# Another tile ring for the weights' transfers, and a later split, in a four-layer cross-attention kernel

## The chip, the cores and the metric

The kernel runs on one NeuronCore of one Trainium2 chip. The metric is the device time of one execution in microseconds (us), shown as a median of several runs. Work is spread over TensorE (PE; its weight loads are PEld), VectorE (DVE), ScalarE (ACT), GpSimd (POOL) and SyncE (SP), which here issues all transfers. Each engine works through its own list of instructions strictly in order; semaphores hold an instruction back until what it needs is there.

## The reference

Four transformer layers in a row work on `x` (32 batches of 112 rows, 256 wide, float32), and on a context `ctx` (32 x 375 x 256). Cut to what matters:

```python
def L0(x, kv):              # grouped attention, 16 heads of 64, 4 for keys and values
    return x + attend(rms(x) @ wq.T, rms(kv) @ wk.T, rms(kv) @ wv.T) @ wo.T
def L1(x, context):         # heads of 16, everything quantised to 8 bits
    x = attn_q(ln(x), ln(x)) + x
    x = attn_q(ln(x), context) + x
    a, g = split(ln(x) @ ff_w1 + ff_b1)
    return a * gelu(g) @ ff_w2 + ff_b2 + x
def L2(q, k, v):            # 16 heads of 64
    q1 = q + attend(ln(q) @ Wq, k @ Wk, v @ Wv) @ Wproj.T + bproj
    return q1 + relu(ln(q1) @ W1.T + b1) @ W2.T + b2
def L3(x_e, x):             # heads of 16, the first attention causal
    x = x + mha(ln(x), ln(x), causal=True) @ m_proj_w + m_proj_b
    x = x + mha(ln(x), x_e, causal=False) @ c_proj_w + c_proj_b
    return x + relu(ln(x) @ f_w1 + f_b1) @ f_w2 + f_b2
y = L3(ctx, L2(L1(L0(x, ctx), ctx), ctx, ctx))
```

## The kernel before

**Sweeps and slots.** Nine sweeps go over all 32 batches: `l0x`; `l1s`, `l1x`, `l1f`; `l2x`, `l2f`; `l3s`, `l3x`, `l3f` (s is self-attention, x cross-attention, f a feed-forward). `order` lays them out in pairs that overlap (l0x with l1s, l1x with l1f, l2x alone, l2f with l3s, l3x with l3f) as one list of 1672 slots. A slot is a small piece of a sweep: two heads of one batch in l0x, four heads in l3s, one eighth of the inner width for two batches in a feed-forward. `run` goes through the slots by their number k. At each it emits the slot's matrix products and, by `LAGS`, later stages of earlier slots; `fill` places projections, norms and loads ahead of their due slot.

**Two orders.** What `run` emits is a priority, not yet the order. When the program is built, a scheduler replays it against its own estimate of how long everything takes, and lets an instruction go early if its inputs and its tile are free and its engine has nothing more urgent. The result is a fixed list for each engine. `tc.issue_after(ins)` keeps what is traced inside it behind `ins` in the list of the engine that runs `ins`, and concerns no other engine.

**Tiles.** SBUF tiles come from rings, one for each tag, with the number of places given by `BUFS`: `xh` has 4, `s1` has 9, `k3` has 11, `w` (split weights) has 8. A tile of a ring has to wait until an older tile of it is given up. `xh` serves the norms: squares (L443), the normalised rows (L219, L475) and the scaled, transposed rows (L213, L215). `s1` serves the feed-forwards' inner sums `uu` (l1f, l2f, l3f), the quantised probabilities and their transposes in l1s, and the v tiles of l1s and l3s (two for each batch of l3s; L1018 clears them).

**Weights.** Matrix products are done as three passes on a high and a low part, so every weight has to be split. `wtile` (L302 on) cuts a weight into chunks of 128 x 256 float32, 128 KB each. For a chunk, `load` (L318) brings it into a raw tile: of `k3` for the first three weights of layer 0, of `xh` for all others. `cut` writes the high part into the `w` tile (`copy`, L202 on ACT, L204 on DVE or L206 on POOL, chosen by the `SHARE` tables) and the low part by a subtraction (L233, on DVE or POOL); for l3s's and l3x's query weights a scaling (L323) goes first. `run` loads one chunk for each slot (`load_w`) as soon as its `w` tile is free, and splits it (`cut_w`) at the next slot, just before the next load:

```python
                cut_w()
                for z in self.sweeps:
                    if wq[z]:
                        if not wq[z][0][0] or free_w > 0:
                            load_w(z)
                        break
```

By that rule layer 0's, l1s's and the first of l1x's weights are loaded in slots 0 to 31, l2f's 16 chunks in slots 767 to 776 and 1021 to 1028, l3s's and l3x's in 1029 to 1044, and l3f's 16 chunks in slots 1265 to 1280, where l2f ends, l3s runs until 1302 and l3x begins.

**Small loads.** `vec` and `scalar` queue the loads of bias and scale vectors in `self.early`; `vectors(2)` issues two of them for each of the slots 8 to 33, behind the last transfer of queries (`lastq`, L715). `self.then` holds four functions that need them: two of `deltas` (L1366 to L1368: reciprocals and products of quantisation steps, for l1s and l1x) and two scalings of query biases (L1389, for l3s and l3x). All four are emitted at slot 34. `load_biases`, at slot 40, writes a tile of zeros to memory, loads the eight output biases into one `xh` tile (L281), splits it (L282) and combines both parts into `biases`, which later products add with one more pass (L291).

Of the kernel before, what the change touches and what calls it, by code (L numbers as in the profile page):

```python
# [8 lines left out]
F32 = mybir.dt.float32  # L9
F32R = mybir.dt.float32r  # L10
# [11 lines left out]
D = 256  # L22
# [39 lines left out]
class Kern:  # L62
# [5 lines left out]
        l0x=[0, 1, 3, 4, 7],  # L68
        l1s=[0, 1, 3, 4, 5],
# [3 lines left out]
        l2f=[0, 0, 0, 0, 0],  # L73
        l3s=[0, 0, 1, 2, 2],
        l3x=[0, 1, 3, 4, 4],
        l3f=[0, 4, 1, 4, 3],
# [46 lines left out]
    def __init__(self, ctx, tc, A, out, B, sweeps):  # L123
        self.tc, self.nc, self.A, self.out, self.B = tc, tc.nc, A, out, B
        self.sweeps = sweeps
        self.uid = 0
        self.cp = ctx.enter_context(tc.tile_pool(name="cp", bufs=1))
        self.wp = ctx.enter_context(tc.tile_pool(name="wp", bufs=1))
        self.sp = ctx.enter_context(tc.tile_pool(name="sp", bufs=1))
        self.pp = ctx.enter_context(tc.tile_pool(name="pp", bufs=1, space=PSUM))  # L130
        self.dp = ctx.enter_context(tc.tile_pool(name="dp", bufs=1, space=DRAM))
        nc = self.nc
        self.turns, self.cur, self.wait = {}, None, None

        self.early, self.then, self.lastq = [], [], None

        self.dqs = {}
        c = lambda name, shape, dt: self.cp.tile(shape, dt, name=name, tag=name)
        self.ident = c("ident", [128, 128], F32)
        make_identity(nc, self.ident)  # L140
        self.identb = c("identb", [128, 128], BF16)
        make_identity(nc, self.identb)
        self.nhalf = c("nhalf", [128, 4], F32)
        nc.gpsimd.memset(self.nhalf, -0.5)
        self.magic = c("magic", [128, 1], F32)
        nc.gpsimd.memset(self.magic, MAGIC)
        self.evod = c("evod", [128, 2], F32)
        nc.gpsimd.memset(self.evod, 0.0)
        for e in range(2):
            nc.vector.tensor_reduce(  # L150
                self.evod[:, e : e + 1], self.ident.rearrange("p (a b d) -> p a b d", b=2, d=16)[:, :, e, :], AX.XY, ALU.add
            )

        self.biases = c("biases", [128, D], F32R)
        self.parity = c("parity", [128, 2], F32)
        self.pick = c("pick", [128, 8], F32R)
        pick = c("pick_", [128, 8], F32)
        nc.vector.tensor_reduce(pick, self.ident.rearrange("p (n b) -> p n b", b=2)[:, :8, :], AX.X, ALU.add)
        for e in range(2):
            nc.vector.tensor_reduce(self.parity[:, e : e + 1], self.ident.rearrange("p (n b) -> p n b", b=2)[:, :, e], AX.X, ALU.add)  # L160
        nc.vector.tensor_copy(self.pick, pick)

        own = c("own", [128, 8], F32)
        nc.vector.tensor_reduce(own, self.ident.rearrange("p (a d) -> p a d", d=16), AX.X, ALU.add)
        self.own = c("ownb", [128, 8], BF16)
        nc.vector.tensor_copy(self.own, own)
        self.mask = c("mask", [S, S], BF16)
        nc.gpsimd.memset(self.mask, 0.0)
        nc.gpsimd.affine_select(
            out=self.mask, in_=self.mask, pattern=[[-1, S]], base=0, channel_multiplier=1, compare_op=ALU.is_ge, fill=NEG  # L170
        )
# [98 lines left out]
    def load_biases(self):  # L270

        nc = self.nc
        self.zeros = self.dram([128, 8 * S], F32, "zeros", 1)
        z = self.t([128, 8 * S], F32, "h")
        nc.gpsimd.memset(z, 0.0)
        nc.sync.dma_start(self.zeros, z)
        raw, lo = self.t([128, D], F32, "xh"), self.t([128, D], F32, "xh")
        hi = self.t([128, D], F32R, "xh")
        nc.gpsimd.memset(raw, 0.0)
        for n, name in enumerate(self.BIAS.values()):  # L280
            nc.sync.dma_start(raw[2 * n : 2 * n + 2], self.A[name].partition_broadcast(2))  # L281
        self.split(raw, hi, lo)  # L282
        nc.vector.tensor_scalar(raw, hi.bitcast(F32), self.parity[:, 0:1], None, ALU.mult)
        nc.vector.scalar_tensor_tensor(self.biases, lo, self.parity[:, 1:2], raw, ALU.mult, ALU.add)
# [13 lines left out]

    FIRST = tuple("L0_xattn_" + n for n in ("wk", "wv", "wq"))


    def wtile(self, r, *parts):  # L302

        box = {}
        chunks = []
        o = 0
        for pi, (key, src, k0, kc, n0, n, *by) in enumerate(parts):
            by = by[0] if by else 1.0
            for q, m in [(q, m) for q in range(kc) for m in range(0, n, 256)]:

                def load(first=pi == 0 and q == 0 and m == 0, o=o, kc=kc, src=src, k=k0 + q, m=m, n0=n0, n=n):
                    if first:
                        self.uid += 1
                        box["w"] = self.wp.tile([128, 2048], F32R, tag="w", name=f"w_{self.uid}", bufs=self.BUFS["w"])
                    v = box["w"][:, o : o + kc * n * 2].rearrange("p (k h n) -> p k h n", k=kc, h=2)
                    a = self.A[src].rearrange("(k p) n -> p k n", p=128)
                    raw = self.t([128, 256], F32, "k3" if src in self.FIRST else "xh")
                    self.lastw = self.nc.sync.dma_start(raw, a[:, k, n0 + m : n0 + m + 256])  # L318
                    return v, raw

                def cut(v, raw, q=q, m=m, src=src, key=key, done=q == kc - 1 and m + 256 >= n, by=by):
                    if by != 1.0:
                        self.nc.vector.tensor_scalar(raw, raw, by, None, ALU.mult)  # L323
                    hi, lo = v[:, q, 0, m : m + 256], v[:, q, 1, m : m + 256]
                    if src in self.PARITY:
                        raw = raw.rearrange("p (m j d) -> p j d m", j=2, d=16)
                        hi, lo = (z.rearrange("p (j d m) -> p j d m", j=2, d=16) for z in (hi, lo))
                    self.split(raw, hi, lo)
                    if done:
                        r[key] = v  # L330

                chunks.append((load, cut))
            o += kc * n * 2
        return chunks
# [1094 lines left out]
    def run(self):  # L1429
# [61 lines left out]
        free_w = self.BUFS["w"]  # L1491
        held = []

        def cut_w():
            while held:
                f, st = held.pop(0)
                f(*st)

        def load_w(s):
            nonlocal free_w  # L1500
            new, ld, ct = wq[s].pop(0)
            free_w -= new
            assert free_w >= 0, s
            held.append((ct, ld()))

        for s in self.sweeps:

# [28 lines left out]
        def fill(k, share):  # L1536
            nonlocal budget
            budget += share
            while budget > 0:
# [7 lines left out]
                atoms[s].pop(0)[4]()  # L1547
                settle(k, s)

        for k in range(max(max(due), len(slots)) + 1):  # L1550
            if 8 <= k < 34:
                self.vectors(2)
            if k == 34:
                self.vectors()
                for f in self.then:
                    f()
            if k == 40:
                cut_w()
                self.load_biases()
            free_w += free_at.get(k, 0)  # L1560
            for s in self.sweeps:
                settle(k, s)
            need, parts = 0.0, 3
            if k < len(slots):
                s, ui, sl = slots[k]
                while s and atoms[s] and atoms[s][0][0] <= k:
                    assert all(self.have_x(s, b) for b in atoms[s][0][5]), (s, ui)
                    self.cur = s
                    atoms[s].pop(0)[4]()
                cut_w()  # L1570
                for z in self.sweeps:
                    if wq[z]:
                        if not wq[z][0][0] or free_w > 0:
                            load_w(z)
                        break
                acc, parts = 0.0, self.PARTS.get(s, 3)
                for d, c, _ in ahead(k):
                    acc += c
                    need = max(need, acc / max(1, d - k))
                budget = min(budget, 0.0)  # L1580
                self.cur = s
                sl.st[0]()
            fill(k, need / parts)
            for q in range(1, 5):
                for j in [j for e, j in due.get(k, []) if e == q]:
                    self.cur = slots[j][0]
                    f = slots[j][2].st[q]
                    if f:
                        f()
                if q in (2, 3):  # L1590
                    fill(k, need / parts)
# [77 lines left out]
```

## Time and profile before

| | us |
|---|---|
| median of 3 runs | 4806.71 |
| lowest, highest | 4796.98, 4807.12 |
| the profiled execution | 4799.79 |
| its span, first to last instruction | 4797.7 |

| stage (us) | PE busy | DVE busy | granted clock | DMA share | what runs |
|---|---|---|---|---|---|
| 0 to 20 | 3.35 | 5.62 | 1.00 | 0.53 | first loads, norms |
| 20 to 60 | 33.78 | 20.59 | 0.91 | 0.43 | l0x |
| 60 to 100 | 33.15 | 24.88 | 0.91 | 0.44 | l0x |
| 400 to 1000 | 581.12 | 493.86 | 1.00 | 0.36 | l0x and l1s, steady |
| 3980 to 4000 | 13.87 | 8.78 | 0.77 | 0.73 | l3s ends, l3x begins |
| 4000 to 4020 | 13.71 | 13.81 | 0.91 | 0.83 | the same |

The busy time of a stage is the time in which the engine was at work, so 33.78 us in a stage of 40 leave 6.22 us of idle time. The granted clock is the share of full speed that PE had; the DMA share is the mean busy share of the core's 16 DMA engines. In an answer in order of time, a line gives the start, the length, the engine, the line of the kernel, the operation, out<-in by tile names, shapes, how many were merged, and in brackets how long the engine had been idle before it and whose signal ended that. A releaser named "DMA xh<-..." is a transfer's landing.

### The profile page before, as it was taken

To read this page: it belongs to the slowest core of one execution; us is meant where nothing else is said; L and a number is where in the kernel's file an instruction comes from. 1 tells how busy PE (TensorE), PEld (TensorE's weight loads), DVE (VectorE), ACT (ScalarE), POOL (GpSimd) and SP (SyncE) were. 2 spreads that over 40 slices of the span, in tenths; PEclk is the share of its full clock that TensorE was granted. 3 is DMA by queue.
4 is the path that set the end of the run, shared out by engine and by line. 5 is a ranking of instruction groups with operands and counts; after the bars stand their busy time and mean duration, and the time that the engine had idled before them with its cause. 6 is when DMAs were issued, how large, how long until landed. Compare 5 with 4: busy or idle time off the path is not lost.

```text
span 4797.7 us, 111165 instructions
## 1 busy us (share of the span) xinstructions
PE 4449.6 (93%) x37824; PEld 3960.6 (83%) x37824; DVE 3619.7 (75%) x9803; ACT 3412.9 (71%) x10645; POOL 2131.3 (44%) x3676
## 2 busy tenths in 40 slices
PE   7999999998778999999999999999999997899999
PEld 6888888887667888887999999998899986778888
DVE  5788888888888888887688888888566655677776
ACT  5788888887767777775577777775555554677776
POOL 5455455556444343333233333334444443566665
PEclk9999999999889999999999999999999997899999
DMA  4433333334665565566355445543777777666663
GB/s 109 125 87 88 82 86 82 83 84 120 139 132 136 147 144 147 145 153 160 108 144 144 138 140 140 146 142 103 198 218 220 221 201 207 159 165 166 164 166 84
DMA packets 590020, 674.50 MB, mean 141 GB/s; under 512 B 331488, under 2 KB 499664, under 8 KB 589264
## 3 DMA queue, kind: packets, MB, share of 16 engines
q1 hardware_dynamic: 589456, 667.38, 54.6%
q8 instruction: 305, 5.00, 0.5%
q14 instruction: 259, 2.12, 0.1%
HBM read 323.55 MB, written 173.02 MB: 104 GB/s over the span
## 4 chain that ended last, share of the span: by engine, by line
PE 42%; DVE 5%; DMA 4%; ACT 1%; issue 1%; POOL 1%; SPq 0%; ACTq 0%; DVEq 0%; POOLq 0%
PE ps L698 7%; PE ps L237 6%; PE ps L238 5%; PE ps L239 5%; PE sc L807 3%; PE ps L829 3%; PE ps L1130 3%; PE sc L1166 2%; PE acc L237 2%; PE acc L239 1%; PE acc L238 1%; PE ps L1294 1%; DVE sm L640 1%; PE ps L1240 1%; DMA k<-k 1%
## 5 line engine op out<-in xcount | busy, mean ns | idle before, releaser
L219 POOL TENSOR_SCALAR k<-k,sm 112x375 f32<-112x375 f32 (+1 forms) x1536 | 941.7, 626 | 1054.1 <-DVE sm L680 474.5
L202 ACT ACTIVATE k<-ps 125x336 f32<-125x336 f32 (+4 forms) x2005 | 916.3, 470 | 419.8 <-PE ps L239 185.2
L640 DVE TENSOR_REDUCE sm<-sc 112x1 f32<-112x375 f32 x1792 | 945.1, 539 | 150.7 <-PE sc L807 86.6
L646 ACT ACTIVATE k<-sc,sm 112x375 f32<-112x375 f32 x1536 | 881.9, 580 | 103.3 <-DVE sm L640 79.9
L698 PE MATMUL ps<-ident,k 112*125 112x112 f32 x4608 | 736.4, 278 | 20.4 <-issue 4.0
L698 PEld LDWEIGHTS ps<-ident,k 112*125 112x125 f32 x4608 | 653.5, 191 | 76.0 <-issue 45.7
L807 PE MATMUL sc<-k,qs 128*112 128x376 f32 x2048 | 540.7, 357 | 21.4 <-ACT k L646 11.4
L237 PE MATMUL ps<-w,k 128*125 128x256 f32 (+2 forms) x1344 | 426.3, 317 | 32.0 <-ACT k L646 17.4
L729 DVE TENSOR_TENSOR k<-ps,k 64x376 fp32r<-64x376 f32 x640 | 350.3, 547 | 121.7 <-ACT k L202 106.5
L237 PE MATMUL ps<-h,w 128*128 128x224 f32 x1408 | 408.8, 297 | 34.6 <-DVE h L204 13.0
L204 DVE COPY k<-ps 125x336 f32<-125x336 f32 (+2 forms) x619 | 289.7, 468 | 152.3 <-PE ps L239 60.2
L238 PE MATMUL ps<-h,w 128*128 128x224 f32 x1408 | 394.0, 282 | 2.6 <-POOL h L233 2.0
L239 PE MATMUL ps<-h,w 128*128 128x224 f32 x1408 | 393.2, 282 | 1.3 <-POOL w L233 1.2
L238 PE MATMUL ps<-w,k 128*125 128x256 f32 (+2 forms) x1344 | 385.6, 287 | 0.0
L239 PE MATMUL ps<-w,k 128*125 128x256 f32 (+2 forms) x1344 | 384.7, 286 | 0.0
L829 PE MATMUL ps<-k,k 125*64 125x112 f32 (+1 forms) x4608 | 351.9, 297 | 1.6 <-ACT k L202 1.3
L215 POOL TENSOR_SCALAR k<-k,sm 112x375 f32<-112x375 f32 x256 | 165.8, 648 | 416.8 <-DVE sm L680 314.9
L237 PE MATMUL ps<-k,w 128*128 128x376 f32 x896 | 336.5, 376 | 15.2 <-ACT k L646 5.8
L807 PEld LDWEIGHTS sc<-k,qs 128*112 128x112 f32 x2048 | 305.3, 177 | 50.7 <-ACT k L646 24.9
L237 PEld LDWEIGHTS ps<-w,k 128*125 128x125 f32 (+2 forms) x1344 | 258.8, 193 | 82.5 <-ACT k L646 30.3
L646 ACT ACTIVATION_READ_ACCUMULATOR k<-sc,sm 112x1 f32 x1536 | 323.7, 211 | 0.0
L237 PEld LDWEIGHTS ps<-h,w 128*128 128x128 f32 x1408 | 272.4, 197 | 56.8 <-issue 18.2
(216 smaller groups left out, 12559.6 us busy)
## 6 DMA issues: line engine op xcount, KB each, us to landing
qs<-h SPq DMA_DIRECT2D x512, 224.0 KB
k<-k SPq DMA_DIRECT2D x192, 376.0 KB
k<-cd SPq DMA_DIRECT2D x64, 752.0 KB
vd<-k SPq DMA_DIRECT2D x128, 375.0 KB
k<-vd SPq DMA_DIRECT2D x128, 375.0 KB
qs<-dq_l3s SPq DMA_DIRECT2D x128, 224.0 KB
qs<-dq_l3x SPq DMA_DIRECT2D x128, 224.0 KB
x<-xd SPq DMA_DIRECT2D x224, 112.0 KB
```

The costliest lines, as they stand in the source:

```text
L202: self.nc.scalar.activation(out, in_, AF.Identity)
L204: self.nc.vector.tensor_copy(out, in_)
L219: self.nc.gpsimd.tensor_scalar(out, in_, by, 1.0, ALU.mult, ALU.mult)
L237: mm(out, lhs(0), rhs(0), start=start, stop=False)
L238: mm(out, lhs(0), rhs(1), start=False, stop=False)
L239: mm(out, lhs(1), rhs(0), start=False, stop=stop)
L640: nc.vector.tensor_reduce(nms[j], sc[j][:, :n], AX.X, ALU.max, negate=True)
L646: nc.scalar.activation(p[:, j, :n], sc[j][:, :n], AF.Exp, bias=nms[j], scale=1.0 if scale is None else scale, accum_out=sm[:, j : j + 1])
L698: self.nc.tensor.transpose(pst[:TB, a * S : (a + 1) * S], p[:, j, a * TB : (a + 1) * TB], self.ident[:S, :S])
L729: nc.vector.tensor_tensor(ks[o, j, :], pk[r, :TE], ks[r, j, :].bitcast(F32), ALU.subtract)
L807: nc.tensor.matmul(sc[:, :TE], qs[:, hd, q, bs], kk, start=q == 0, stop=q == 1)
L829: nc.tensor.matmul(o if gqa else o[:, mm, :], vq[:, a, hd * 64 : hd * 64 + 64], st["pt"][:, :, j, ta] if gqa else st["pt", mm][:, j, ta], ...
```

## The change

It does five things:

- A weight's raw tile comes from `s1` and not from `xh`, if it is loaded before slot 50 or belongs to `w1` or `w2` of layer 2 or 3 (l2f and l3f). The first three weights of layer 0 keep `k3`; l1x's other weights, l2x's, and l3s's and l3x's keep `xh`.
- A chunk's split carries the slot at which it may be emitted: three slots behind its load for l0x, l1s, l2f and l3f, one slot for the others. Splits stay in the order of their loads.
- `load_biases` is emitted at slot 32 (its raw tile from `s1`); the split, now `cut_biases`, at slot 44. Before, both stood at slot 40, behind a flush of all splits.
- Vector loads go out in slots 6 to 31 instead of 8 to 33.
- Of the four functions in `then`, the first stays at slot 34 and the other three go to slot 60, inside an `issue_after` on `lastq`.

```diff
-                    raw = self.t([128, 256], F32, "k3" if src in self.FIRST else "xh")
+                    raw = self.t([128, 256], F32, "k3" if src in self.FIRST else "s1" if self.idle(src) else "xh")
...
+    def idle(self, src):
+
+        return self.slot < 50 or src in ("L2_xattn_w1", "L2_xattn_w2", "L3_xattn_w1", "L3_xattn_w2")
...
-        raw, lo = self.t([128, D], F32, "xh"), self.t([128, D], F32, "xh")
-        hi = self.t([128, D], F32R, "xh")
+        raw = self.t([128, D], F32, "s1")
         nc.gpsimd.memset(raw, 0.0)
         for n, name in enumerate(self.BIAS.values()):
             nc.sync.dma_start(raw[2 * n : 2 * n + 2], self.A[name].partition_broadcast(2))
+        return raw
+
+    def cut_biases(self, raw):
+        nc = self.nc
+        hi, lo = self.t([128, D], F32R, "xh"), self.t([128, D], F32, "xh")
         self.split(raw, hi, lo)
...
-        def cut_w():
-            while held:
-                f, st = held.pop(0)
+        def cut_w(k=None):
+            while held and (k is None or held[0][0] <= k):
+                _, f, st = held.pop(0)
                 f(*st)
...
-            held.append((ct, ld()))
+            st = ld()
+            held.append((self.slot + (LATER if s in ("l0x", "l1s", "l2f", "l3f") else 1), ct, st))
...
+        LATER = 3
         for k in range(max(max(due), len(slots)) + 1):
-            if 8 <= k < 34:
+            self.slot = k
+            if 6 <= k < 32:
                 self.vectors(2)
-            if k == 34:
+            if k in (34, 60):
+                with self.tc.issue_after(self.lastq.ins):
+                    for f in self.then[:1] if k == 34 else self.then[1:]:
+                        f()
+            if k == 32:
                 self.vectors()
-                for f in self.then:
-                    f()
-            if k == 40:
-                cut_w()
-                self.load_biases()
+                biases = self.load_biases()
+            if k == 44:
+                self.cut_biases(biases)
...
-                cut_w()
+                cut_w(k)
```

More of the change, by code (lines that the diff above doesn't have):

```diff
@@ L133, in __init__ @@
         self.turns, self.cur, self.wait = {}, None, None
-        self.early, self.then, self.lastq = [], [], None
+        self.early, self.then, self.lastq, self.slot = [], [], None, 0
         self.dqs = {}
```

## The prediction

> **What bounds the kernel now.** I read the page first (busy shares, the forty slices), then the busy time by stage, then the instructions in order of time wherever a stage falls behind.
>
> ```profile
> PE 4449.6 (93%) x37824; PEld 3960.6 (83%) x37824; DVE 3619.7 (75%) x9803; ACT 3412.9 (71%) x10645; POOL 2131.3 (44%) x3676
> PE   7999999998778999999999999999999997899999
> PEclk9999999999889999999999999999999997899999
> ```
>
> TensorE (PE) is the bound: 93%, and nine tenths nearly everywhere. Time can only come from slices where PE idles: the first one, around 1200 us, and slices 33 and 34, around 4000 us. The change touches the first and the last, so I cut those into stages (columns: length, busy time of PE, PEld, DVE, ACT, POOL, granted clock, DMA share, GB/s).
>
> ```profile
> 3850.00:3900.00 50.00, 49.63 (x445) 45.85 (x443) 29.65 (x83) 30.08 (x122) 18.64 (x34) 1.00 0.79 217
> 3900.00:3920.00 20.00, 20.00 (x183) 18.35 (x182) 10.83 (x31) 12.92 (x56) 9.04 (x16) 1.00 0.87 247
> 3920.00:3940.00 20.00, 11.31 (x76) 10.72 (x76) 7.59 (x26) 3.52 (x13) 5.21 (x8) 0.74 0.35 107
> 3940.00:3960.00 20.00, 19.73 (x177) 17.41 (x176) 15.41 (x38) 13.27 (x56) 10.69 (x22) 1.00 0.95 265
> 3960.00:3980.00 20.00, 10.83 (x78) 9.21 (x76) 8.43 (x24) 7.26 (x32) 5.49 (x8) 0.72 0.77 216
> ```
>
> Until 3920 us PE has no hole. Then every engine is half idle, DMA too in the third row: something is waited for. VectorE (DVE) and PE in order of time say what:
>
> ```profile
> 3933.19 0.29 DVE L204 CAST w<-xh 128x256 fp32r<-128x256 f32 x1 [10.83 <-DMA xh<-in_L_xattn_w_dram]
> 3970.68 0.29 DVE L204 CAST w<-xh 128x256 fp32r<-128x256 f32 x1 [4.32 <-DMA xh<-in_L_xattn_w_dram]
> 4016.40 0.66 DVE L204 CAST w<-xh 128x256 fp32r<-128x256 f32 x2 [3.24 <-DMA xh<-in_L_xattn_w_dram]
> ...
> 3933.77 0.56 PE L291 MATMUL ps<-biases,pick 128*112 128x256 f32 x1 [8.41 <-ACT pp L202]
> 3973.80 0.61 PE L477 MATMUL ps<-ident,xh 112*128 112x112 f32 x2 [6.47 <-DVE xh L475]
> 4019.44 0.65 PE L1166 MATMUL sc<-k,qs 128*112 128x376 f32 x1 [4.97 <-ACT k L646]
> ```
>
> These are splits of l3f's weights (load L318, high half L202/L204/L206, low half L233). The split stands in DVE's and ScalarE's (ACT's) own order in front of l3s's and l3x's work; the transfer has not landed; all behind it stops, and PE idles 8.41 + 6.47 + 4.97 = 19.85 us. SP's queue issued the first of these loads at 3921.09, so it took over 11 us to be usable; others took 9.0 (3961.69 to 3970.68) and, at 2321 us, 2.4 (2321.32 to 2323.72).
>
> The start has the same kind of wait behind small transfers:
>
> ```profile
> 70.96 0.16 DVE L1366 RECIPROCAL iq<-s_L_xattn_d_q 128x1 f32<-128x1 f32 x1 [3.26 <-DMA s_L_xattn_d_q<-in_L_xattn_d_q_dram]
> 92.75 0.16 DVE L1366 RECIPROCAL iq<-s_L_xattn_d_q 128x1 f32<-128x1 f32 x1 [1.35 <-DMA s_L_xattn_d_q<-in_L_xattn_d_q_dram]
> 130.42 0.17 DVE L1389 TENSOR_SCALAR vec_L_xattn_cq_b<-vec_L_xattn_cq_b 128x2 f32<-128x2 f32 x1 [2.81 <-DMA vec_L_xattn_cq_b<-in_L_xattn_cq_b_dram]
> 191.62 0.29 DVE L204 CAST xh<-xh 128x256 fp32r<-128x256 f32 x1 [4.66 <-DMA xh<-in_L_xattn_f_b_dram]
> ```
>
> PE's idle times just behind them are 4.46 us (at 75.50), 1.31 (94.88), 1.84 (131.09) and 2.78 + 1.14 (195.19, 196.67).
>
> **How far a traced place binds.** The scheduler fixes each engine's order ahead, by its own estimate of times, and may pull ready work forward. The first L1366 is traced at slot 34; before 70.9 us PE had run 46 of L807, four to a slot, so it ran in slot 12. A later traced place is therefore a lower priority, not a guarantee, and I credit such moves in part.
>
> **The sum, part by part**, against the profiled execution (4799.79 us, of which 4797.7 is the span):
>
> 1. *l3f's splits, three slots behind the load instead of one.* From 3700 to 3900 us PE ran 157 of L1219, four per l3s slot: 39 slots; l2f has as many, so a slot lasts 200 / 78 = 2.55 us and two more slots are 5.1 us. That covers 5.1 + 5.1 + 4.97 = 15.2 of the 19.85 us. Late next are l3x's and l3s's own transfers: PE idles 5.82 us at 3989.16 for k<-dk and 8.03 at 4092.22 for dq_l3x, and DMA is at a share of 0.73 from 3921 to 4020. I take half, -7.6. Bounds: -19.9, and +10, if 16 loads of 128 KB brought forward (2 MB at 207 GB/s) all stand ahead of those.
> 2. *The clock in these holes.* Granted 0.74 and 0.72 in two of the 20 us rows: 5.2 + 5.6 us of full clock missing, with PE busy 55% of them, 6 us. Two of three holes shrink: -3 (0 to -6).
> 3. *l2f's weights through s1.* PE idles 1.03 + 1.10 us at 2337 and 2340, and 3.69 at 3296.43 behind the split of l3s's wq, which keeps xh but finds it emptier. I take -3 (0 to -5.8).
> 4. *Biases loaded at slot 32, split at 44.* Eight loads at 181.59 to 187.10, the last waited for 4.66 us. From 130 to 190 us PE ran 66 of L807: 3.6 us a slot, so 12 slots are 43 us, if they hold. Of 3.92 us I take -3 (0 to -3.9).
> 5. *Second deltas and the two L1389 from slot 34 to 60.* Of 1.31 + 1.84 us, -2 (0 to -3.2). The ordering put around them binds SP's queue and they are DVE instructions, so it moves nothing. The first deltas (4.46 us) stay at 34: 0. Vectors from slot 6 instead of 8 only change which qs transfer they queue behind: 0, hidden by PE's own work between such transfers.
> 6. *First loads through nine s1 tiles instead of four xh.* SP issued four of wo at 14.73 to 17.07; now up to nine can go: five times 128 KB at the 140 GB/s of the first 20 us is 4.6 us, ahead of qs<-h, for which PE idles 1.38 and 1.42 us at 28.57 and 30.56. SP has nothing to issue from 17.44 to 23.97, which is their cover; without it the 4.6 is lost. The later wait of 3.83 us on wo at 59.98 costs PE nothing visible. I take +1 (-2.8 to +4.6).
>
> No instruction is added or removed: tags and places change, and every L318, L204 and L233 keeps its row's duration (0.38, 0.29, 0.74 us). Sum: -7.6 - 3 - 3 - 3 - 2 + 1 = -17.6, so 4782 on the profiled execution. The median of the runs shown (4806.71) is 6.9 above that execution, the lowest 2.8 below; on the median it would be 4789. I say **4786**.
>
> The Trainium skill speaks against term 1: "DMA: Bandwidth & Descriptors", section "Anatomy of one DMA — SWDGE (gpsimd) path", puts a transfer at some 2.0 us fixed plus bytes at 436 GB/s, an estimate of 2.3 us for 128 KB (it was fitted on transfers that GpSimd issues; these are SP's). By it one slot is enough and term 1 is nothing, the sum about -10. The row at 2321 us (2.4) agrees with it, those from 3921 us on (over 11, 9.0) do not, and the rows decide. For term 2, "TensorE: Matmul & The Clock Gate", Part 1, says the clock is halved after an idle window of about 3.4 us and needs as long to return; by that three holes are worth an estimated 5 us, my bound's upper part.
>
> **Rivals.** (a) *Slower: s1 isn't idle when l3f's weights come.* l3s's v tiles (two a unit) live there: L1018 clears ten of them from 3918 to 3966 us, five units in 48 us, and a pair lives some nine l3s slots (lead 3, 4 slots, lag 2) of 5.1 us, 46 us. That is ten tiles for nine places before the first weight. If more than nine are wanted, v's copy waits for a weight's split, and that for its transfer: a new hole of the kind of 8.41 us, for each of the four groups of four loads, 34 us, less the 19.85 that go and with +1 from the start: 4799.8 + 34 - 19.85 + 1 = 4815, on the median 4822. Against it: tiles are cleared early because they stand free. (b) *DMA takes over.* Share 0.95 from 3940 to 3960 us; each hole saved is idle before k<-dk or qs<-dq_l3x, terms 1 and 2 vanish: -7, 4793 profiled, 4800 median: within 0.2%. (c) *The change doesn't do what it says*: the scheduler pulls splits, deltas and biases forward as it does L1366, waits stay, +1: about 4801, 4808 median.
>
> **Chances.** Forecast 0.58, (a) 0.22, (b) 0.10, (c) 0.10. About 0.2% (9.6 us) is what a measurement can tell from no change: faster 0.58, same 0.20, slower 0.22. All lower bounds together are -41.6, so 4758; half the way from the sum to there is 4770, and the forecast's own range is 4770 to 4797. With (a) to (c) the range for 8 in 10 is **4758 to 4826**: the lower bounds, and (a) with four us over it for the orders that a new plan may shuffle.
>
> **What would show it.** Right: DVE's and ACT's waits for w_dram between 3920 and 4020 us under 8 us in all (now 19.9 and 13.9), PE busy over 77 of these 100 us (now 69.5); no 4.66 at the biases. (a): DVE or ACT waiting to write s, or POOL's L1018, behind w L233. (b): PE's idle time moves to DMA k<-dk and qs. (c): the same waits with s in place of xh. Wrong altogether if a stage that nothing here touches, such as 400 to 1000 us, moves by more than 5 us: then the reordering itself is the effect.

## The result and the profile after

The changed kernel is a little slower: median 4811.15 us (22 runs, 4801.51 to 4829.22) against 4804.28 for the kernel before (22 runs), ratio 1.0017 [1.0010, 1.0025], some +8 us. The time lies inside the predicted range, on the other side of no change than forecast. The profiled execution took 4820.78 us, so single executions of one kernel differ by more than most of the effects here. I therefore mostly read *lags*: the start of the n-th matmul of a PE line less the start of the same matmul in the profile of before. Between two points where nothing was changed a lag should stay level. It does so within some 2 us: e1, e11 and e12 below have the lists of the kernel before on PE, VectorE, ACT and POOL up to 1000 us, and their lags at 347 us are -0.5, -1.7 and -1.6.

| reading of lag, us | changed kernel |
|---|---|
| at 347 us of before (layer 0 steady, start over) | +8.4 |
| gained or lost from 347 to 1035 us | +1.6 |
| 1035 to 2214 (l1x, l1f) | +14.9 |
| 3257 to 3412 (l2f into l3s) | -2.3 |
| 3895 to 4144 (l3f's weights) | -1.4 |

The third row is no effect whose cause I can name: from 1229 to 2321 us VectorE's list is the same in both kernels, and the lag creeps. It is not mere scatter either. In the eight profiles with the start's tiles in `s1` (the changed kernel, e2, e5, e6, e7, e9, e13, e16) this row is +8.4 to +18.0, on average 14.0; in the nine others it is +2.8 to +12.0, on average 7.0. How tiles of the first 50 slots could act there no run shows. The first, fourth and fifth rows are where the change acts directly: +8.4 - 2.3 - 1.4 = +4.7, against +5 to +12 from the interval of the ratio, so a part of the third row may belong to the change as well.

From the changed kernel's page, busy time and the forty slices of PE and its clock:

```profile
PE 4460.2 (93%) x37824; PEld 3967.0 (82%) x37824; DVE 3622.9 (75%) x9805; ACT 3409.6 (71%) x10645; POOL 2122.2 (44%) x3674
...
PE   7999999998778999998999999999899996899999
...
PEclk9999999999888999999999999999999997899999
```

The dip around 4000 us is still there, in the same two slices. VectorE's sums of waits (total us, times, longest) at l3f's weights, before and then after, tell that the waits for weights did go:

```profile
DVE w L204 <- DMA xh<-in_L_xattn_w_dram: 19.9, 4, 10.8
```

```profile
DVE w L204 <- DMA s<-in_L_xattn_w_dram: 4.8, 4, 2.7
```

ACT's 13.9 us of the same are gone altogether. PE in order of time in the changed kernel shows what came in their place:

```profile
3976.04 1.72 PE L1227 MATMUL sc<-k,qs 128*112 128x112 f32 x8 [3.66 <-DMA k<-dk]
...
4002.50 0.57 PE L1227 MATMUL sc<-k,qs 128*112 128x112 f32 x4 [3.67 <-DMA k<-dk]
...
4014.08 1.25 PE L1174 MATMUL sc<-k,qs 128*112 128x376 f32 x3 [7.25 <-DMA x<-xd]
...
4037.42 0.65 PE L1174 MATMUL sc<-k,qs 128*112 128x376 f32 x1 [5.78 <-ACT k L654]
```

The ACT instruction before the last of these rows had itself waited 4.94 us for DMA k<-k. The same piece of work as one stretch each, before and after (length, PE, PEld, DVE, ACT, POOL, clock, DMA share, GB/s):

```profile
3900.00:4144.00 244.00, 186.00 (x1551) 160.83 (x1550) 132.88 (x368) 124.46 (x472) 91.91 (x149) 0.80 0.73 195
```

```profile
3924.00:4167.00 243.00, 187.02 (x1552) 159.94 (x1551) 132.15 (x371) 123.82 (x473) 92.40 (x149) 0.82 0.74 196
```

244 us against 243 us: the holes at the weights closed, others opened at transfers of l3s and l3x, and the stretch is no shorter. That is the sign of rival (b) of the prediction. Whether the DMA's rate itself sets the length is not shown: with the same 47.58 MB in the same time the two rates (195 and 196 GB/s) have to agree, and in rows of 20 us the DMA share goes from 0.35 to 0.95 before (3920 to 3960 us) and from 0.51 to 0.93 after (3940 to 3980 us). The prediction's own sign of being right is half there: VectorE's and ACT's waits are 4.8 us in all, under its 8, but PE was busy for 73.3 of the 100 us from 3944 on, not for over 77.

The start is where time was lost. VectorE in order of time, and below it PE:

```profile
61.94 0.16 DVE L1374 RECIPROCAL iq<-s_L_xattn_d_q 128x1 f32<-128x1 f32 x1 [8.82 <-DMA s_L_xattn_d_q<-in_L_xattn_d_q_dram]
...
81.06 0.16 DVE L1374 RECIPROCAL iv<-s_L_xattn_d_v 128x1 f32<-128x1 f32 x1 [2.11 <-DMA s_L_xattn_d_v<-in_L_xattn_d_v_dram]
...
131.63 0.17 DVE L1397 TENSOR_SCALAR vec_L_xattn_cq_b<-vec_L_xattn_cq_b 128x2 f32<-128x2 f32 x1 [1.31 <-DMA vec_L_xattn_cq_b<-in_L_xattn_cq_b_dram]
```

```profile
63.78 1.59 PE L815 MATMUL sc<-k,qs 128*112 128x376 f32 x4 [5.71 <-ACT k L654]
```

VectorE stands 8.82 us at the first reciprocal of the deltas (3.26 before), and PE 5.71 us behind it (4.46 before). VectorE got there at 53.1 us; SP issued the load of d_q only at 57.14. The 4.66 us wait on the biases at 191 us is gone. Another loss is quieter: from 40 to 60 us.

```profile
40.00:60.00 20.00, 13.86 (x77) 10.14 (x75) 12.22 (x30) 11.43 (x34) 19.36 (x33) 0.91 0.66 173
```

PE was busy for 13.86 us of these 20 (17.33 before), POOL for 19.36 (10.92 before).

### The profile page after: what moved, and what is told of

Its sections match the earlier page's. It is cut to its first block, busy times and chain, and to the rows that moved or that the text cites. A ratio compares the mean times of both kernels' runs of the same rounds, so it can differ in the third digit from the quotient of the medians.

```text
span 4819.0 us, 111177 instructions
## 1 busy us (share of the span) xinstructions
PE 4460.2 (93%) x37824; PEld 3967.0 (82%) x37824; DVE 3622.9 (75%) x9805; ACT 3409.6 (71%) x10645; POOL 2122.2 (44%) x3674
## 5 line engine op out<-in xcount | busy, mean ns | idle before, releaser
L654 ACT ACTIVATE k<-sc,sm 112x375 f32<-112x375 f32 x1536 | 882.1, 580 | 128.5 <-DVE sm L648 87.8
L237 PE MATMUL ps<-h,w 128*128 128x224 f32 x1408 | 409.1, 297 | 29.1 <-DVE h L204 13.9
L654 ACT ACTIVATION_READ_ACCUMULATOR k<-sc,sm 112x1 f32 x1536 | 323.7, 211 | 0.0
L837 PEld LDWEIGHTS ps<-k,k 125*64 125x64 f32 x4608 | 248.5, 137 | 81.2 <-issue 18.8
```

The costliest lines, as they stand in the source:

```text
L237: mm(out, lhs(0), rhs(0), start=start, stop=False)
L654: nc.scalar.activation(p[:, j, :n], sc[j][:, :n], AF.Exp, bias=nms[j], scale=1.0 if scale is None else scale, accum_out=sm[:, j : j + 1])
L837: nc.tensor.matmul(o if gqa else o[:, mm, :], vq[:, a, hd * 64 : hd * 64 + 64], st["pt"][:, :, j, ta] if gqa else st["pt", mm][:, j, ta], ...
```

## The experiments

Ratios are to the kernel before on the same chip; e1 to e4 and e9 to e12 ran on one chip, e5 to e8 on another, e13 to e16 on a third. "Lag" is that at 347 us. Where a kernel ran once, its time says nothing at this scale and only its profile is read.

| run | what | ratio | lag | 3257 to 3412 | 3895 to 4144 |
|---|---|---|---|---|---|
| changed kernel | all | 1.0017 [1.0010, 1.0025] | +8.4 | -2.3 | -1.4 |
| e1 | feed-forward part alone | 0.9991 [0.9981, 1.0001] | -0.5 | -4.0 | -1.6 |
| e2 | start's tiles and splits alone | 1.0010 [1.0000, 1.0021] | -0.5 | +0.9 | -2.3 |
| e3 | biases alone | 1.0002 [0.9991, 1.0014] | -3.1 | +0.3 | -0.2 |
| e4 | vector loads and functions alone | 1.0011 [1.0001, 1.0020] | +3.2 | +0.6 | -2.4 |
| e5 | changed, without e4's part | 0.9988 [0.9979, 0.9997] | -1.5 | -4.4 | -5.3 |
| e6 | e2 and e4 | one run, 4834.72 us | +14.6 | -0.1 | +0.1 |
| e7 | e2 and e3 | one run, 4809.23 us | -3.7 | +0.3 | +1.6 |
| e8 | e4 and e3 | one run, 4804.10 us | -4.4 | -0.3 | +0.9 |
| e9 | changed, functions held | 0.9986 [0.9975, 0.9996] | -3.7 | -5.1 | -0.7 |
| e10 | e1 and e3, functions held | **0.9958 [0.9946, 0.9969]** | -9.6 | -4.6 | -2.8 |
| e11 | feed-forward weights in s1 alone | one run, 4797.06 us | -1.7 | -3.9 | -4.8 |
| e12 | their later split alone | one run, 4792.68 us | -1.6 | 0.0 | +2.0 |
| e13 | e10 and s1 at the start | 0.9973 [0.9963, 0.9983] | -4.8 | -4.3 | -2.8 |
| e14 | e10 and later splits at the start | 0.9970 [0.9958, 0.9982] | -10.7 | -5.9 | -4.7 |
| e15 | e10 and vectors from slot 6 | 0.9988 [0.9978, 0.9997] | +0.7 | -5.1 | -1.7 |
| e16 | e13 and e14 | 0.9980 [0.9971, 0.9989] | -5.3 | -6.7 | -5.0 |

The last column moves by over 2 us also where the feed-forward part is absent (e2, e4), and by as much when it is read one matmul later (e5 -3.2, e9 +0.9), so single entries of it are no finer than 2 to 3 us.

### The four parts alone: e1 to e4

Each is the kernel before with one part of the change.

```diff
# e1: tiles and later splits of l2f and l3f only
+        return src in ("L2_xattn_w1", "L2_xattn_w2", "L3_xattn_w1", "L3_xattn_w2")
+            held.append((self.slot + (LATER if s in ("l2f", "l3f") else 1), ct, st))
# e2: tiles before slot 50, later splits of l0x and l1s only
+        return self.slot < 50
+            held.append((self.slot + (LATER if s in ("l0x", "l1s") else 1), ct, st))
# e3: load_biases at 32, cut_biases at 44
# e4: vector loads in 6 to 31, the functions at 34 and 60
```

> Before, with only the weights of l2f and l3f moved to s1 and split three slots behind. Theory 1 (the changed kernel's loss is made in the first 100 us, its gain at the feed-forwards' weights is small because the transfers there take over): the first L807 matmuls up to 1000 us at the times of before, within 0.5 us; splits' waits near 3930 us gone; whole kernel 3 to 8 us faster. Theory 2 (the loss is a chance of reordering, spread over the kernel): 0 to 4 us slower, with no stage that stands out. The rival of the prediction (v tiles crowd s1): 5 us or more slower, made after 3920 us.

> Before, with only the weights loaded before slot 50 moved to s1 and split three slots behind for l0x and l1s. Theory 1a (the early loads and their splits crowd POOL and DVE at 35 to 60 us): 5 to 9 us slower, nearly all of it by 100 us, PE's busy time from 20 to 60 us some 3 us under before's 33.8. Theory 1b (the small vector loads make the loss, not the weights): within 2 us of before at 250 us.

> Before, with only the output biases loaded at slot 32 through s1 and split at slot 44. Theory 1: DVE's wait of 4.66 us at 191 us is gone and the lag at 250 us is -2 to -4 us; whole kernel 2 to 4 us faster. Theory 2: within 1 us at 250 us, since the scheduler pulls the split forward to where it thinks the loads have landed.

> Before, with only the vector loads two slots earlier and three of the four small functions at slot 60. Theory 1b (these make the loss: the first reciprocal of the deltas moves forward with its load and DVE waits for it for 8 us): 4 to 8 us slower at 100 us. Theory 1a: within 2 us of before at 250 us, since the waits for d_q only change place.

The biases give their -3.1 us of lag, the feed-forward part its -4.0 at l2f and only -1.6 at l3f. The vector part loses 3.2 us. The ratios hardly show any of this: only e4's interval leaves out 1, and by 0.0001. The sum of the four lags, -0.5 - 0.5 - 3.1 + 3.2 = -0.9, is far from the +8.4 of all together: two parts must harm each other.

### Which two: e5 to e8

```diff
# e5: the changed kernel with e4's part undone
-            if 6 <= k < 32:
+            if 8 <= k < 34:
...
-            if k in (34, 60):
+            if k == 34:
```

e6, e7 and e8 are the kernel before with two parts each (see the table).

> The changed kernel with one part undone: vector loads from slot 8 and all four small functions at slot 34, as before. Alone, the parts moved the PE's work at 347 us by -0.5 (weights before slot 50), -3.1 (biases) and +3.2 us (vectors), together by +8.4, so some pair interacts by 8.8 us. If the pair has the vectors in it: -3 to -4 us at 347 us, and the whole kernel 4 to 8 us faster than before. If it is weights and biases: +5 us or more at 347 us, and no gain.

> Before with the weights before slot 50 through s1 and the vectors' part. Theory A (the early weights let DVE reach the first reciprocal of the deltas earlier, while their loads queue behind weights and later loads): +8 to +12 us at 347 us, with a wait of 6 us or more of DVE for d_q. Theory B (other pairs): +2.7 us, the sum of the two.

> Before with the weights before slot 50 through s1 and the biases' part. Theory A: -3.6 us at 347 us, the sum of the two. Theory C (the biases' raw tile and the weights share s1, and the early biases' eight loads delay layer 0's): +3 us or more.

> Before with the vectors' and the biases' parts. Theory A: +0.1 us at 347 us, the sum of the two. Theory D (vectors two slots earlier and biases eight slots earlier crowd SP's queue together): +5 us or more.

It is the start's tiles with the vector part: +14.6 where the two alone add to +2.7. The other pairs don't harm each other; e7's -3.7 is the sum of its parts (-3.6), e8's -4.4 is better than its own (+0.1), by more than I can explain. Without the vector part the changed kernel is faster than the kernel before (e5). VectorE in e6:

```profile
65.12 0.17 DVE L1370 RECIPROCAL iq<-s_L_xattn_d_q 128x1 f32<-128x1 f32 x1 [9.56 <-DMA s_L_xattn_d_q<-in_L_xattn_d_q_dram]
```

PE's next wait there is 7.88 us, at 66.80. The place of that reciprocal in VectorE's list, counted in instructions as built, tells a part of why:

```
                      iq1   iq2   mq_b  cq_b
kernel before          83   125    153   179
changed kernel         66   105    148   173
e5 (vectors from 8)    98   123    153   179
e9, e10 (held)        232   404    410   411
```

With the loads from slot 6 the scheduler places the first reciprocal 17 instructions earlier. That alone does not cost the 9 us: e4 has it at the same place (the 69th instruction of VectorE in its trace, the 68th in the changed kernel's) and waits there for only 0.24 us. The tiles change what stands ahead of it. In the changed kernel and e6 these are 16 casts of weights and 12 maxima of the softmax, in e4 9 casts and 15 maxima. In the changed kernel VectorE was through with them at 53.1 us, 4 us before the load's issue (57.14); in e4 at 60.0 us, 3 us after it (56.76). The earlier loads brought the second pair and the two query biases forward too, although these are now traced at slot 60 and not at 34.

### Holding the functions back: e9 and e10

`issue_after` is now given an instruction of VectorE, the last maximum of the softmax (`mark_v`), in place of a transfer of SP. e9 is the changed kernel with that; e10 is the kernel before with e1's and e3's parts and that.

```diff
-            nc.vector.tensor_reduce(nms[j], sc[j][:, :n], AX.X, ALU.max, negate=True)
+            self.mark_v = nc.vector.tensor_reduce(nms[j], sc[j][:, :n], AX.X, ALU.max, negate=True)
...
-                with self.tc.issue_after(self.lastq.ins):
+                with self.tc.issue_after(self.mark_v.ins):
```

> The changed kernel, but its four small functions (deltas, query bias scalings) are held behind a maximum of the softmax of slot 33 or 59 in VectorE's own list. In that list the first reciprocal stands at place 232 (66 in the changed kernel, 83 in the kernel before), the second pair at 404 (105 and 125). Theory A (the reciprocals pulled forward in VectorE's list, ahead of the landing of d_q, are what the start loses): VectorE's wait of 8.82 us for d_q and PE's 5.71 us behind it are gone, as are the 2.11 to 1.00 us waits at 81 to 99 us and 1.31 us at 132; the lag against the kernel before at its 347 us goes from +8.4 to between -6 and 0, and the time to about 4796, ratio to before 0.996 to 0.999. Theory B (the loads in SP's queue and the fuller DMA cost it, whoever waits for them): a wait of like size turns up at another load or at x, the lag at 347 us stays over +4 and the ratio at 1.001 or above.

> The kernel before with the feed-forward part (tiles of s1, splits three slots later for l2f and l3f), the biases at 32 and 44, and the four small functions held in VectorE's list as in e9; layer 0's and l1's weights and the vector loads as before. If the parts that showed a gain add up (feed-forward -0.5 and biases -3.1 us at 347 us, up to 4.46 + 1.31 + 1.84 us of PE's idle time behind the small transfers, -4 at l2f/l3s): lag -5 to -11 at 347 us, -8 to -15 after l2f, time 4790 to 4797, ratio 0.997 to 0.999. Theory B: small transfers are waited for elsewhere, lag at 347 us about -3.6, ratio 0.999 to 1.000.

In e10 the reciprocal runs at 160 us and waits for nothing:

```profile
160.19 0.14 DVE L1374 RECIPROCAL iq<-s_L_xattn_d_q 128x1 f32<-128x1 f32 x1
```

In e9, too, no wait of VectorE for a delta or a query bias is left; the lag falls from +8.4 to -3.7, and the ratio from 1.0017 to 0.9986. So the reciprocals are where the start lost its time: holding them and the other small functions back is worth 12 us of lag. About half of it the kernel before pays as well: in e10 the same is worth some 6 us (-9.6, where e1's and e3's parts alone give -0.5 and -3.1). e10 is the fastest kernel of the study: 4784.66 us beside 4807.01 for the kernel before. But e9 lacks some 13 us against e10, and that was still to be explained.

### Tiles or later split at the feed-forwards: e11 and e12

```diff
# e11: as e1 with every split one slot behind its load
# e12: as e1 with tiles of xh
-                    raw = self.t([128, 256], F32, "k3" if src in self.FIRST else "s1" if self.idle(src) else "xh")
+                    raw = self.t([128, 256], F32, "k3" if src in self.FIRST else "xh")
```

> The kernel before with l2f's and l3f's weights in tiles of s1 alone; splits one slot behind their load as before. If the later split removes the waits: VectorE's waits for w_dram from 3920 to 4040 us stay over 12 us (19.9 before, under 6 in the changed kernel), PE's holes too, and the stage 3895 to 4144 us gains under 1.5 us. If the nine places do it, by letting loads go out earlier: waits under 8 us, the stage as in e1 (-1.6). In both, l2f/l3s (3257 to 3412) gains about 4 us as in e1.

> The kernel before with l2f's and l3f's splits three slots behind their loads, tiles of xh (four places) as before. If the later split removes the waits: VectorE's waits for w_dram from 3920 to 4040 us under 8 us, and the stage 3895 to 4144 us -1 to -5. If three held chunks of four places starve the norms, which share xh: PE or ACT waits for xh, the stage +2 to +15. l2f/l3s (3257 to 3412) then gains nothing or loses (the chunks stay longer in xh ahead of mwq).

VectorE in e12, the later split alone:

```profile
3932.42 0.29 DVE L204 CAST w<-xh 128x256 fp32r<-128x256 f32 x1 [10.47 <-DMA xh<-in_L_xattn_w_dram]
...
3968.41 0.29 DVE L204 CAST w<-xh 128x256 fp32r<-128x256 f32 x1 [3.36 <-DMA xh<-in_L_xattn_w_dram]
...
3997.56 0.29 DVE L204 CAST w<-xh 128x256 fp32r<-128x256 f32 x1 [4.29 <-DMA xh<-in_L_xattn_w_dram]
```

With 2.50 and 0.45 us more, 21.1 us on VectorE (19.9 before). ACT's 13.9 us are gone, but POOL's went from 3.8 to 13.1, and PE's three holes of 8.41, 6.47 and 4.97 us are still 7.93, 6.40 and 4.74 us: two slots later in the traced order change next to nothing. e11 has 10.6 on VectorE and 4.4 on ACT, e1 with both 8.0 and none, and PE's longest hole in e11 is 5.99 us, for k<-dk. So it is the tiles that take most of the waits away, which I had not credited; neither of the two bounds set for e11 (over 12, under 8) held. The l2f gain is the tiles' alone, too (-3.9 and 0.0). SP's issues show what the tiles change, in the kernel before and then in e1:

```profile
3919.62 0.38 SPq L876 DMA_DIRECT2D k<-k  x1
3920.16 0.83 SPq L555 DMA_DIRECT2D v<-k  x2
3921.09 0.84 SPq L318 DMA_DIRECT2D xh<-in_L_xattn_w_dram  x2
```

```profile
3937.57 0.93 SPq L322 DMA_DIRECT2D s<-in_L_xattn_w_dram  x2
```

Before, the first two loads stand right behind some 1.1 MB of k and v (375 and 376 KB each), and their splits start 11.7 us after the issue (3932.86 and 3933.19); the DMA was busy for a share of only 0.2 to 0.4 from 3923 to 3930 us, so it is not a full DMA that held them. In e1 they go out 16 us later, not earlier, behind smaller transfers (112 KB each), and are split at 3939.83 and 3940.61. Why the scheduler puts them there with tiles of `s1` I have not traced.

### What e9 lacks against e10: e13 to e16

Each is e10 with something of the start put back.

```diff
# e13, e16
-        return src in ("L2_xattn_w1", "L2_xattn_w2", "L3_xattn_w1", "L3_xattn_w2")
+        return self.slot < 50 or src in ("L2_xattn_w1", "L2_xattn_w2", "L3_xattn_w1", "L3_xattn_w2")
# e14, e16
-            held.append((self.slot + (LATER if s in ('l2f', 'l3f') else 1), ct, st))
+            held.append((self.slot + (LATER if s in ('l0x', 'l1s', 'l2f', 'l3f') else 1), ct, st))
# e15
-            if 8 <= k < 34:
+            if 6 <= k < 32:
```

> e10 with one part put back: all weights loaded before slot 50 that are not in k3 take tiles of s1 (nine), as in the changed kernel. Theory A (the early tiles cost): the transfers that they let go early fill the DMA between 14 and 60 us and stand ahead of small loads; lag at 347 us +3 to +7 against e10 (-9.6 there), the later drift from 1136 to 2215 us larger too (+7 to +15 in the six profiles that have this part, 0 to +5 in those that have neither it nor the earlier vector loads), time +8 to +15 us, ratio to before 0.9975 to 0.9995. Theory B (term 6 of the prediction, +1): lag at 347 us within 2 us of e10, ratio 0.995 to 0.997.

> e10 with one other part put back: the splits of l0x's and l1s's weights three slots behind their loads instead of one, tiles of xh as before. If this is what costs: xh's four places are held longer, norms wait, lag at 347 us +3 or more against e10, ratio 0.9975 or above. If not: within 2 us, ratio 0.995 to 0.997, since a place in the order that is only a priority moves splits little.

> e10 with the vector loads from slot 6 instead of 8; the four small functions stay held in VectorE's list. Theory A (the loads cost only because the reciprocals follow them forward): within 2 us of e10 at 347 us, ratio 0.995 to 0.997. Rival (26 small loads two slots earlier hold up queries and contexts in SP's queue by themselves): lag at 347 us +2 to +6 against e10, ratio 0.9965 to 0.998.

> e10 with both parts at the start put back (tiles of s1 before slot 50, splits three slots later for l0x and l1s): the changed kernel but for the vector loads from slot 8 and the four functions held. If the start part is what e9 (0.9986) lacks against e10 (0.9958), this comes out near e9, 0.998 to 0.9995; if the earlier vector loads are, near e10, 0.995 to 0.997.

**e15, the vector loads: +10.3 us of lag**, more than the rival's +2 to +6, though no reciprocal waits. POOL, PE and SP in order of time:

```profile
68.61 0.40 POOL L206 CAST w<-xh 128x256 fp32r<-128x256 f32 x1 [7.58 <-DMA xh<-in_L_xattn_wo_dram]
```

```profile
69.63 0.97 PE L706 MATMUL ps<-ident,k 112*125 112x112 f32 x3 [4.77 <-POOL k L219]
```

```profile
54.52 1.09 SPq L252 DMA_DIRECT2D vec_L_xattn_ln_g<-in_L_xattn_ln_g_dram  x1
55.65 0.94 SPq L252 DMA_DIRECT2D vec_L_xattn_ln_b<-in_L_xattn_ln_b_dram  x1
56.63 0.47 SPq L326 DMA_DIRECT2D xh<-in_L_xattn_wo_dram  x1
57.14 0.43 SPq L299 DMA_DIRECT2D s_L_xattn_d_q<-in_L_xattn_d_q_dram  x1
57.62 0.43 SPq L299 DMA_DIRECT2D s_L_xattn_d_k<-in_L_xattn_d_k_dram  x1
58.15 0.29 SPq L606 DMA_DIRECT2D k<-in_ctx_dram  x1
58.48 0.52 SPq L326 DMA_DIRECT2D xh<-in_L_xattn_wo_dram  x1
```

Four small loads now go out ahead of a context and a chunk of wo; that chunk is usable 10.1 us after its issue (58.48 to 68.61). In e10 two chunks of wo had gone out at 54.19, ahead of any small load. So the small loads cost by themselves where wo is still to come (e4 and e8 show the same wait, 6.13 and 6.77 us; in both, PE's hole of 4.46 us behind the first reciprocal is gone at the same time, and e8's lag is even -4.4). Of the 10.3 us, 7.4 are there at 80 us; the rest comes by 200 us and I have not traced it. In the changed kernel all of wo has been issued by 19.8 us, into s1, and it is the reciprocal that pays instead.

**e13, the tiles at the start: +4.8 us of lag**, ratio 0.9973 against 0.9958 (on another chip, and the intervals overlap). POOL's groups from 40 to 60 us (count, busy us and mean ns, idle before), in e13 and then in e10:

```profile
L233 POOL TENSOR_TENSOR w<-s,w 128x256 fp32r<-128x256 f32 x17 | 12.4, 750 | 0.6 <-DVE w L204 0.6
...
L233 POOL TENSOR_TENSOR w<-k,w 128x256 fp32r<-128x256 f32 x2 | 1.5, 726 | 0.0
```

```profile
L233 POOL TENSOR_TENSOR w<-xh,w 128x256 fp32r<-128x256 f32 x3 | 2.3, 765 | 1.3 <-DVE w L204 1.3
L233 POOL TENSOR_TENSOR w<-k,w 128x256 fp32r<-128x256 f32 x3 | 2.2, 729 | 0.2 <-DVE w L204 0.2
```

Nineteen low halves in place of six: weights that have landed early are split early, POOL is full, and so nearly is VectorE. The same 20 us of both, in e13 and then in e10:

```profile
40.00:60.00 20.00, 13.78 (x88) 10.48 (x86) 17.46 (x37) 12.47 (x38) 19.36 (x33) 0.99 0.67 180
```

```profile
40.00:60.00 20.00, 16.95 (x102) 14.44 (x101) 11.86 (x29) 12.42 (x38) 10.66 (x19) 0.83 0.53 130
```

PE does 3.2 us less in it; its waits there end with ACT's normalised rows (k, L654), 1.34, 1.27 and 2.15 us at 46.86, 52.41 and 59.56, and ACT in turn waits for VectorE's maxima, 5.7 us in these 20 us against 2.6 in e10. Part comes back when POOL has nothing left to split after 80 us. I had looked for the price in the DMA; this chain puts it on VectorE. What POOL adds is not separated. Of the 5.6 us by which VectorE is busier, 3.07 are one 112 x 2 instruction (L470 at 55.65 us, median 0.17 us over the kernel) that runs while POOL works without a pause; why it took so long is not shown. Nor is the price the same in every kernel: e2 has the same crowd (eighteen low halves, POOL 19.36 us) and a lag of -0.5, perhaps because its first reciprocal waits for 1.38 us instead of 3.26. The later row, 1035 to 2214 us, is +14.1 here and +5.4 in e10, as the expectation had it (+7 to +15).

**e14, the later splits: nothing shown.** Its lag is the best of all (-10.7), its ratio not told apart from e10's. e16 has e13's lag. Of e9's 13 us against e10, the lags explain 5.9 (e9 -3.7, e10 -9.6), and the tiles alone most of that. In the two profiles the row from 1035 to 2214 us holds 12 more (+17.5 and +5.4). By the grouping above that goes with the start's tiles, but its cause stays open, and the two ratios are no finer than some 5 us each way.

## Why the prediction was wrong

**Part 5, and in it the two zeros: the step that failed most.** "The first deltas (4.46 us) stay at 34: 0" and "Vectors from slot 6 instead of 8 only change which qs transfer they queue behind: 0, hidden by PE's own work". I had written myself that a traced place is a priority, and still took the place of the reciprocals as given. The list is made by estimates, loads earlier in the trace let the scheduler put the reciprocal at 66 instead of 83, and with the tiles of part 6 VectorE stands there before the load of d_q has even been issued. This part measured +9.9 us of lag (+8.4 with it, -1.5 without) where I had -2. Together with parts 1 and 2, -1.4 where I had -10.6, that is 21 of the some 26 us between my sum (-17.6) and the result (some +8). The remark that the ordering binds SP only, and not VectorE, was right, and e9 shows what binding VectorE is worth.

**Part 1, half right in effect, wrong in cause.** The waits on weights went (19.9 and 13.9 us to 4.8 and 0), as far as "under 8" asked. But e12 shows that the later split does next to none of it, and the 15.2 us that I worked out from two slots of 2.55 us have no ground; the tiles move the loads in SP's queue. And the time went as in rival (b), to which I gave 0.10: -7.6 and the clock's -3 (part 2) became -1.4, give or take 2 to 3 us. The step that failed is "I take half": PE's next waits, for k<-dk, x<-xd and k<-k, took the whole gain. The clock in the stretch rose from 0.80 to 0.82 with PE's busy time up 1 us.

**Part 3** (-3) measured -2.3, and -4.0 in e1: right, by the tiles. **Part 4** (-3) measured -3.1 of lag in e3, and the wait of 4.66 us is gone: right, though e3's ratio (1.0002) doesn't show it.

**Part 6** (+1, -2.8 to +4.6) is near nothing alone (e2's lag -0.5), +4.8 in e13, and with part 5 some 12 more than the two alone (e6). The size was off and the cause too: I weighed five transfers in front of qs, and not the splits that each early weight brings, nor that they let VectorE reach an instruction before its data.

**Rival (a)**, a shortage of s1's places in l3s, showed its sign only in small: POOL's clearing of a v tile (L1026, L1018 before) waits behind a weight's split for 1.35 us at 3964.13 and 0.34 us at 4018.43, which it did not before. The four holes of 8.41 us did not come, and the stage loses nothing. So (a) named the side on which the time came out by a mechanism that did not bring it there, and that the time lies inside the range, whose upper end was (a)'s, is luck. **Rival (c)** held for one part only: deltas and biases of queries stayed pulled forward, weights didn't.

My test for "wrong altogether", a move of over 5 us from 400 to 1000 us, was not met (under 2). A better one would have been the place of each moved instruction in its engine's list, and what stands ahead of it there.

The rule of the Trainium skill that I set against part 1 ("DMA: Bandwidth & Descriptors", some 2.3 us for 128 KB as an estimate) was right for the load itself: e1's first loads are split 2.3 to 2.5 us after their issue (3937.57 and 3938.10). The 9 to 11 us that I let decide were those of loads in another place of the queue, the first two right behind 1.1 MB, and two slots more did not cover them (e12).

## What to carry to other kernels

A moved line of the program is a hint to the scheduler; ask where the instruction lands in its engine's list, and bind it to an instruction of that same engine if it must not come early. Loads brought forward bring their consumers with them: price these (here the splits on POOL and VectorE, the reciprocals on VectorE), and the small transfers that now stand ahead of large ones. Before a hole is booked as gain, look for the wait that ends next behind it: here the holes at the weights closed and the stretch took 243 us instead of 244.

## What the runs showed of the hardware

In e15 the transfers issued behind four small loads started later than the loads' bytes explain. The DMA's share and rate over 58 to 62 us of that run, in forty slices of 0.1 us:

```profile
DMA  6997543111000000000000000000000000000269
GB/s 114 299 308 205 72 51 31 10 21 11 0 0 0 0 1 0 1 0 0 0 0 0 0 0 0 0 0 0 0 0 0 0 0 0 0 0 1 62 185 430
DMA packets 545, 0.18 MB, mean 45 GB/s; under 512 B 385, under 2 KB 544, under 8 KB 544
```

From 59.0 to 61.6 us nothing moves, though 375 KB of context and 128 KB of wo have been issued since 58.15 and 58.48; only 0.18 MB pass in the 4 us, and most packets are under 512 B. The Trainium skill, "DMA: Bandwidth & Descriptors", section "Rules for kernel authors", says that a load whose last dimension isn't contiguous becomes one descriptor per element; the vector loads are of that kind, and the count of small packets agrees with it. Why the DMA then stands still, and does not only move slowly, no run here shows.
